# Graph attention and two graph convolutions on one Trainium2 core: block sums moved on GpSimd, batch 15's lower block sums moved to VectorE, batch 14's last step by seven products

## The chip, the cores and the metric

The kernel runs on one core of a Trainium2 chip (trn2). A core has TensorE (the matrix engine, PE in the profile, with weight loads as PEld), VectorE (DVE), ScalarE (ACT), GpSimd (POOL) and SyncE (SP), which here issues nearly all DMAs. The metric is the device time of one execution in microseconds. All data are float32.

## The reference

For 16 batches of x (1024 nodes, 256 channels) and one dense 1024 x 1024 matrix `adj`:

```python
c_adj = mean of x over channels                          # per node
A     = 2*| |sigmoid(c_adj[m]-c_adj[n]) - 0.5| - 0.5 |   # symmetric in n, m
g     = relu((x^T @ (adj * A)) * para)                   # [256, 1024], per batch
q     = g^T in 4 heads;  k, v = x @ kv_w
att   = softmax(q k^T * scale) v
x1    = layernorm(x + att)
h     = relu(x1 @ w1_loop + adj @ (x1 @ w1_neigh) + b1)  # 128 wide
h     = relu(h @ w2_loop + adj @ (h @ w2_neigh) + b2)    # 256 wide
out   = layernorm(x1 + 0.5*(x1 + h))
```

The last layernorm is over x1 + (x1 + h)/2; the kernel computes it as x1 + h/3 with the epsilon scaled to match.

## The kernel before

Each batch passes three stages on different turns of the loop over b, so that three or four batches are under way at once: the attention of batch b; the adjacency products of batch b+1 for its queries (`q`, class FastQueries); and the two convolutions. A GraphConv object stands for a batch whose attention is done: `c1` is batch b-1, `c2` is b-2, `c3` is b-3. The class Joined takes the first convolution's product of `c1` and the second one's of `c2` as one product with the same `adj`.

Where two 2 x 2 blocked matrices are multiplied, the kernel uses a scheme of seven products instead of eight (Winograd's form). It needs sums of blocks of each factor. Those concerned here are:

- `FastQueries.left` (L604 to L610): four sums of blocks of x, tiles `S`, 128x512 each, for the query products L647 of the next batch; its engine is an argument.
- `Joined.left` (L1120 to L1129): four sums, tiles `R`, for the joined product L1134. The first reads only `h1` of c2; the other three read `t`, the result of c1's small product (L857, copied from PSUM by ScalarE at L860).
- `GraphConv.block_sums` (L953 on): sums of blocks for the last step of c2, which multiplies [u, h1] by the weights w2 (L971, seven groups of four matmuls, `last_products`). Its first sum (L958) and the sum `uT` of the lower half (L1174) run on GpSimd, the rest on VectorE. The sums of the weights come by a DMA, `load_sums` (L950), which is issued from `Joined.run` after the second product.

Before the change the last pass (c1 of batch 15 and c2 of batch 14, after the loop) runs the joined product without `block_sums`, and then `c2.last()`: 16 matmuls of 256 columns into two PSUM tiles (`outer`, L926 and L928) and four long VectorE steps (`residual`, L933 and L936). `ending` then reuses these two PSUM tiles (`filled`) for batch 15.

All is in an order written by hand: an engine runs its instructions in the order of the program. Tiles named "row" (128 x 1024) rotate among 31 addresses: a new tile gets the address that was given back longest ago, and its first writer waits until the last readers of the former tile are done. So the order in which tiles are taken in the program sets which former tile a new one waits for. PSUM has three tiles of two banks ("big", of which `half_psum` uses one half) and two of one bank (`bank_psum`). Batch tiles of x rotate among three addresses (`xpool`): the load of batch 15's x1 (`c1.load_x`, L850) waits until the output of batch 12 (L1018) has left its tile.

In a steady batch (b = 2 to 14) the order around the change is: softmax sums of units 0 and 1 on VectorE (`collect` L721 and L723, `partial` L728 to the tile `accB`, L731 to `den_part`), `both.fetch`, the outputs of both units on PE (L744), `q.left`, the statistics of c3, the sums K of the next keys (L423 to L431), the adj loads, `c1.inner` (`t`), `both.left`, `both.run`.

In batch 15 `both.run` also holds batch 15's own normalisation: its power on GpSimd (L361) is put before the lower block sums.

Of the kernel before, what the change touches and what calls it, by code (L numbers as in the profile page):

```python
# [18 lines left out]
def kernel(  # L19
# [31 lines left out]
    nc = tc.nc  # L51

    B, N, C = x.shape
# [6 lines left out]
    FB = 512  # L60
# [781 lines left out]
    class GraphConv:  # L842
# [51 lines left out]
            nc.sync.dma_start(out=self.h1.rearrange("p (t f) -> p t f", f=HID),  # L894
                              in_=self.h1d.rearrange("(t p) f -> p t f", p=P))

        def turn(self, j):

            if j == 0:
                self.h1 = row_tile(f"h1_{self.b}")  # L900
            pt = half_psum(f"h1n_ps_{self.b}_{j}")
            for i in range(TJ):
                nc.tensor.transpose(pt[:, ts(i, P)], self.h1T[:, ts(j * TJ + i, P)], ident)
            nc.scalar.copy(self.h1[:, ts(j, FB)], pt)
# [45 lines left out]
            nc.sync.dma_start(out=self.w2[:, 0:5 * P], in_=w2_sums)  # L950
            self.b2_step = self.w2[:, ts(4, P)]

        def block_sums(self, base, lower):  # L953
            s12, s34 = (row_tile(f"last_{self.b}_{k}") for k in range(2))
            self.low, self.up = self.uT[:, FB:N], self.uT[:, 0:FB]
            s1, s2, s3, s4 = s12[:, 0:FB], s12[:, FB:N], s34[:, 0:FB], s34[:, FB:N]
            lower()
            nc.gpsimd.tensor_add(s1, self.h1T[:, FB:N], self.low)  # L958
            base()
            nc.vector.tensor_sub(s2, s1, self.up)  # L960
            nc.vector.tensor_sub(s4, self.h1T[:, 0:FB], s2)
            nc.vector.tensor_sub(s3, self.up, self.low)
            t1, t2, t3, t4 = (self.w2[:, ts(n, P)] for n in range(4))
            self.factors = {1: (self.up, w2n_sb[:, ts(0, P)]), 2: (self.h1T[:, 0:FB], w2l_sb[:, ts(0, P)]),
                            3: (s4, w2l_sb[:, ts(1, P)]), 4: (self.h1T[:, FB:N], t4), 5: (s1, t1), 6: (s2, t2), 7: (s3, t3)}
# [137 lines left out]
    class Joined:  # L1103
# [30 lines left out]
                nc.tensor.matmul(dst, self.x[n][:, k, :], of_rows(rows, k),  # L1134
                                 start=(start and k == 0), stop=(k == TJ - 1), skip_group_check=again)

        def run(self, between=None, last=False):
            c1, c2, b = self.c1, self.c2, self.b
            between = between or {}

            def bias(bank, row):
                nc.scalar.copy(bank.rearrange("p (t c) -> p t c", c=P), row.unsqueeze(1).to_broadcast([P, TJ, P]))

            def turn_to(n):
                for f in between.get(n, ()):
                    f()

            first, third, second = (half_psum(f"hu_ps_{b}_{i}") for i in range(3))
            s12, s34 = (row_tile(f"snap_{b}_{k}") for k in range(2))
            p1, u1, u3, p7 = s12[:, 0:FB], s12[:, FB:N], s34[:, 0:FB], s34[:, FB:N]  # L1150
            c1.loop(third, 0, start=True)
            self.product(1, first, start=True)
            nc.scalar.copy(p1, first)
            turn_to(1)
            self.product(2, third)
            nc.vector.tensor_add(p1, p1, third)
            turn_to(2)
            if last:
                bias(third, b2_sb[:, ts(0, P)])
                c2.load_sums()  # L1160
            self.product(6, first, again=True)
            nc.scalar.copy(u1, first)
            c1.relu(0, p1)
            turn_to(6)
            self.product(7, second, start=True)
            nc.scalar.copy(p7, second)
            turn_to(7)
            self.product(5, first, again=True)
            nc.scalar.copy(u3, first)
            turn_to(5)  # L1170
            self.product(4, second, again=True)
            c2.uT = row_tile(f"uT_{c2.b}")
            add_upper = lambda: nc.vector.tensor_add(c2.uT[:, 0:FB], u1, second)
            add_lower = lambda: nc.gpsimd.tensor_add(c2.uT[:, FB:N], u3, p7)  # L1174
            if not last:
                add_upper()
                add_lower()
                turn_to(4)
                c1.loop(first, 1, again=True)
                self.product(3, first, again=True)  # L1180
                c1.relu(1, first)
                turn_to(3)
                return
            c2.block_sums(add_upper, add_lower)
            bias(second, c2.b2_step)
            turn_to(4)
            c1.loop(first, 1, again=True)
            self.product(3, first, again=True, steps=range(0, TJ // 2))
            rest = c2.last_products(third, second)
            self.product(3, first, again=True, steps=range(TJ // 2, TJ))  # L1190
            c1.relu(1, first)
            rest()
            turn_to(3)

    def run():

# [57 lines left out]
        for b in range(B):  # L1254
# [39 lines left out]
            elif more and not both:  # L1294
                att.scores(0)
                att.outputs(0)
                NodeSums(q, xb, str(b + 1)).all()
                kv = KeysValues(b + 1, channel_major(blocked, f"xT_{b + 1}"))
                att.scores(1)
                kv.sums()  # L1300
                att.add(0)
                att.outputs(1)
                for t in (0, TJ):
                    q.load(t)
                c1.inner()
                q.left(nc.gpsimd)
                for t in (0, TJ):
                    q.likeness(t)
                for ij, n in QUARTERS.items():
                    store(n, quarters[ij])  # L1310
                c1.first(quarters, lambda: (att.add(1), adj_sums(quarters, 1), adj_sums(quarters, 2), weigh_first()))
                c1.turn_blocks()
                att.scores(2)
                att.outputs(2)
                for t in (1, TJ + 1):
                    q.load(t)
                    q.likeness(t)
                    q.times_adj(t)
                att.scores(3)
                for t in (2, TJ + 2, 3, TJ + 3):  # L1320
                    q.load(t)
                for t in (2, TJ + 2, 3, TJ + 3):
                    q.likeness(t)
                q.right(1)
                att.add(2)
                att.outputs(3)
            elif more:
                att.both_scores(0, summed=False)
                nodes = NodeSums(q, xb, str(b + 1))
                att.collect(1, 1, 2, 3)  # L1330
                nodes.turn()
                att.collect(1, *range(4, NT))
                att.partial(1)
                both.fetch("00", "10")
                c2.load_x()

                def next_xT():
                    ready["xT"] = channel_major(blocked, f"xT_{b + 1}")

                two_units(0, before_second=next_xT)  # L1340
                q.left(nc.gpsimd)
                if c3:
                    c3.statistics()
                kv = KeysValues(b + 1, ready["xT"])
                kv.sums()
                both.fetch(2, 3)
                nodes.line()
                both.fetch(1)
                nodes.row()
                for t in (0, TJ):  # L1350
                    q.load(t)
                both.fetch(4, "11")
                c1.inner()
                both.left(nc.gpsimd)
                both.run({1: (lambda: q.likeness(0),),
                          2: (lambda: att.add(0, 1), lambda: q.likeness(TJ), lambda: c3 and c3.deviation(), weigh_first)},
                         last=True)
                c1.turn_blocks()
                att.both_scores(1)
                order = (1, TJ + 1, 2, TJ + 2, 3, TJ + 3)  # L1360
                for t in order:
                    q.load(t)
                for t in order:
                    q.likeness(t)

                def weigh_second():
                    q.times_adj(1)
                    q.times_adj(TJ + 1)
                    q.right(1)

                two_units(1, before_second=weigh_second)
            else:
                att.both_scores(0)
                two_units(0)
                att.both_scores(1)
                two_units(1, before_second=lambda: att.add(0, 1))
# [58 lines left out]
            else:  # L1435
# [3 lines left out]
                both.left(nc.gpsimd)  # L1439
                both.fetch(1, 4, "11")  # L1440
                both.run({1: (lambda: att.add(2, 3), att.watch), 6: (norm.mean, norm.squares, norm.sum_squares),
                          5: (lambda: norm.variance(bank_psum),), 4: (norm.scale, norm.spread)}, last=True)
                c1.turn(0)
                c1.turn(1)
            convs[b] = GraphConv(b, norm.x1T, norm.nodes)
# [7 lines left out]
        c4.moments()  # L1453
        c4.finish(out[B - 4])
        c1.load_x()
        both.run({2: (c3.moments,), 7: (lambda: c3.finish(out[B - 3]),), 4: (lambda: c1.turn(0),)})
        filled = c2.last()
        c1.turn(1)
        c2.moments()
        c1.ending(out[B - 1], quarters, lambda: c2.finish_aside(out[B - 2]), filled)  # L1460
# [70 lines left out]
```

## Time and profile before

| | us |
|---|---|
| median of 3 runs (2158.33 to 2158.8) | 2158.66 |
| the profiled execution, whole | 2157.34 |
| its span | 2155.6 |
| a steady batch, start of L361 to start of the next (524.61 to 657.16) | 132.55 |
| PE, first record after product 4 in the last pass to its last matmul of batch 15 (2112.70 to 2146.5) | 33.8 |

The table of slices on the page shows PE and its clock even from end to end:

```profile
PE   9999999999999999999999999999999999999998
...
PEclk9999999999999999999999999999999999999999
DMA  8495765637539275492845929467293672935545
```

The operations that the change touches stand in the costliest groups (line, engine, operation, out<-in, shapes, count | busy us, mean ns of one | idle before them and what ended it):

```profile
L606 POOL TENSOR_TENSOR S<-x 128x512 f32<-128x512 f32 x14 | 25.1, 1794 | 258.2 <-ACT x L286 127.0 <-PE av L744 90.0 <-DMA x1d<-xB_a 23.1
L608 POOL TENSOR_TENSOR S<-x 128x512 f32<-128x512 f32 x14 | 30.6, 2183 | 0.0
L1126 POOL TENSOR_TENSOR R<-R,t 128x512 f32<-128x512 f32 x14 | 17.9, 1276 | 77.9 <-ACT t L860 77.9
L1174 POOL TENSOR_TENSOR uT<-snap 128x512 f32<-128x512 f32 x15 | 22.1, 1473 | 30.6 <-ACT snap L1169 30.6
L958 POOL TENSOR_TENSOR last<-h1T,uT 128x512 f32<-128x512 f32 x14 | 21.7, 1548 | 1.1
```

Idle time of an engine that does not bound the kernel costs nothing by itself; it tells what an instruction waited for.

### The profile page before, as it was taken

To read this page: it belongs to the slowest core of one execution; us is meant where nothing else is said; L and a number is where in the kernel's file an instruction comes from. 1 tells how busy PE (TensorE), PEld (TensorE's weight loads), DVE (VectorE), ACT (ScalarE), POOL (GpSimd) and SP (SyncE) were. 2 spreads that over 40 slices of the span, in tenths; PEclk is the share of its full clock that TensorE was granted. 3 is DMA by queue.
4 is the path that set the end of the run, shared out by engine and by line. 5 is a ranking of instruction groups with operands and counts; after the bars stand their busy time and mean duration, and the time that the engine had idled before them with its cause. 6 is when DMAs were issued, how large, how long until landed. Compare 5 with 4: busy or idle time off the path is not lost. (4 is left out here: it accounts for less than half of the span.)

```text
span 2155.6 us, 25079 instructions
## 1 busy us (share of the span) xinstructions
PE 2121.1 (98%) x8710; PEld 1035.5 (48%) x8710; DVE 1898.0 (88%) x2373; ACT 1138.2 (53%) x1664; POOL 391.8 (18%) x210
## 2 busy tenths in 40 slices
PE   9999999999999999999999999999999999999998
PEld 5344444544444454444554444544445444544454
DVE  6899988989999898998989989899898998989965
ACT  5845535556365563655636556355564546545422
POOL 2010130311303113031130311303022130311021
PEclk9999999999999999999999999999999999999999
DMA  8495765637539275492845929467293672935545
GB/s 220 124 163 199 131 213 138 183 97 151 207 110 268 78 146 192 128 269 69 168 163 135 261 69 198 141 152 235 69 230 109 159 228 69 258 94 120 163 136 179
DMA packets 613573, 346.05 MB, mean 161 GB/s; under 512 B 491968, under 2 KB 556864, under 8 KB 613440
## 3 DMA queue, kind: packets, MB, share of 16 engines
q1 hardware_dynamic: 613168, 344.13, 61.3%
q8 instruction: 70, 1.15, 0.2%
q14 instruction: 63, 0.52, 0.1%
q10 hardware_dynamic: 272, 0.26, 0.0%
HBM read 294.13 MB, written 50.20 MB: 160 GB/s over the span
## 5 line engine op out<-in xcount | busy, mean ns | idle before, releaser
L723 DVE TENSOR_TENSOR acc<-acc,pr 128x1024 f32<-128x1024 f32 x384 | 531.1, 1383 | 37.4 <-DVE acc L723 1.4
L702 PE MATMUL s<-qT,kT 64*128 64x512 f32 x2048 | 449.7, 593 | 0.0
L744 PE MATMUL av<-pr,v 128*64 128x512 f32 x2048 | 447.0, 594 | 0.0
L709 ACT ACTIVATE pr<-s 128x1024 f32<-128x1024 f32 x392 | 390.7, 1115 | 75.6 <-PE s L702 75.6
L702 PEld LDWEIGHTS s<-qT,kT 64*128 64x128 f32 x2048 | 196.3, 187 | 232.7 <-issue 183.3
L361 POOL TENSOR_TENSOR rstd<-rstd,neg_half 128x32 f32<-128x32 f32 x16 | 99.3, 6204 | 1112.7 <-DVE rstd L359 1112.7
L744 PEld LDWEIGHTS av<-pr,v 128*64 128x64 f32 x2048 | 144.0, 137 | 297.3 <-issue 272.6
L1134 PE MATMUL hu_ps<-adj,R 128*128 128x512 f32 x480 | 214.2, 594 | 0.0
L560 ACT ACTIVATE wg<-c_row,c_sums 128x1024 f32<-128x1024 f32 x120 | 137.0, 1142 | 81.4 <-DVE den_part L731 60.3
L566 DVE SCALAR_TENSOR_TENSOR wg<-wg,adj 128x1024 f32<-128x1024 f32 x128 | 149.9, 1210 | 3.6 <-ACT wg L561 3.6
L707 ACT ACTIVATE pr<-s 128x512 f32<-128x512 f32 x240 | 142.4, 702 | 0.3 <-PE s L702 0.3
L1134 PEld LDWEIGHTS hu_ps<-adj,R 128*128 128x128 f32 x480 | 89.1, 190 | 101.4 <-issue 98.3
L561 ACT ACTIVATE wg<-wg 128x1024 f32<-128x1024 f32 x128 | 135.4, 1058 | 4.1
L860 ACT COPY t<-t_ps 128x1024 f32<-128x1024 f32 x16 | 16.2, 1012 | 219.1 <-DVE den_part L731 190.3
L1134 PE MATMUL hu_ps<-adj,t 128*128 128x512 f32 x240 | 108.7, 605 | 21.5 <-ACT t L860 21.5
L647 PE MATMUL g_ps<-wg,S 128*128 128x512 f32 x224 | 115.5, 597 | 0.0
L647 PE MATMUL g_ps<-T,S 128*128 128x512 f32 x224 | 115.5, 597 | 0.0
L647 PE MATMUL g_ps<-wg,x 128*128 128x512 f32 x224 | 109.0, 599 | 0.0
L721 DVE TENSOR_TENSOR acc<-pr,pr 128x1024 f32<-128x1024 f32 x64 | 78.4, 1225 | 12.3 <-ACT pr L709 12.3
L1134 PEld LDWEIGHTS hu_ps<-adj,t 128*128 128x128 f32 x240 | 45.1, 193 | 84.0 <-issue 46.7
L728 DVE STREAM_TRANSPOSE accB<-acc 128x1024 f32<-128x1024 f32 x64 | 79.7, 1245 | 2.2
L731 DVE TENSOR_REDUCE den_part<-accB 128x32 f32<-128x1024 f32 x64 | 78.1, 1220 | 2.2
(239 smaller groups left out, 3062.6 us busy)
## 6 DMA issues: line engine op xcount, KB each, us to landing
adj<-adjT SPq DMA_DIRECT2D x210, 512.0 KB
adj<-in_adj_dram SPq DMA_DIRECT2D x128, 512.0 KB
para<-in_L_gnn_para_dram SPq DMA_DIRECT2D x32, 512.0 KB
xB_a<-in_x_dram SPq DMA_DIRECT2D x128, 128.0 KB
x1d<-xB_a SPq DMA_DIRECT2D x128, 128.0 KB
x<-x1d SPq DMA_DIRECT2D x16, 1024.0 KB
xB<-in_x_dram SPq DMA_DIRECT2D x120, 128.0 KB
x<-in_x_dram SPq DMA_DIRECT2D x15, 1024.0 KB
```

The costliest lines, as they stand in the source:

```text
L361: nc.gpsimd.tensor_tensor(self.rstd, self.rstd, neg_half, ALU.pow)
L560: nc.scalar.activation(wg, self.c_row, AF.Abs, bias=self.c_col[:, t:t + 1], scale=-1.0)
L561: nc.scalar.activation(wg, wg, AF.Tanh, scale=-0.5 / C)
L566: nc.vector.scalar_tensor_tensor(wg, wg, 1.0, self.adj.pop(t), op0=ALU.add, op1=ALU.mult)
L647: nc.tensor.matmul(self.p[n], x_n[:, k, :], w_n, start=(k == 0), stop=(k == TJ - 1))
L702: nc.tensor.matmul(halves[s], self.kT[rows, pair, ts(mt, P)], self.qT[rows, pair, ts(j, FB)], start=True, stop=True)
L707: nc.scalar.activation(pr[:, ts(s, FB)], halves[s], AF.Exp)
L709: nc.scalar.activation(pr, ps, AF.Exp)
L723: nc.vector.tensor_add(self.acc, self.acc, prs[mt])
L728: nc.vector.transpose(accB, self.acc)
L744: nc.tensor.matmul(pav[s * HD:(s + 1) * HD, :], self.v[:, mt, pair * P + s * HD:pair * P + (s + 1) * HD], prs[mt][:, ts(s, FB)], start=(mt ...
L1134: nc.tensor.matmul(dst, self.x[n][:, k, :], of_rows(rows, k), start=(start and k == 0), stop=(k == TJ - 1), skip_group_check=again)
```

## The change

Three edits. In a steady batch `q.left` moves from behind the outputs of units 0 and 1 to behind `both.left`, so GpSimd makes R before S, and the program takes the tiles K, adj, `t` and R before S. In batch 15 the lower sum `uT` and the first block sum go to VectorE (`last` is now the engine of these two). In the last pass the joined product runs with `last=nc.gpsimd`: batch 14's last step goes by `block_sums` and the seven groups of `last_products`, with the weight sums loaded by `load_sums`; `run` hands back its PSUM tiles `third` and `second` in the place of `filled`, and the first turn of h1 takes a one-bank PSUM tile.

```diff
-        def turn(self, j):
+        def turn(self, j, psum_tile=half_psum):
...
-            pt = half_psum(f"h1n_ps_{self.b}_{j}")
+            pt = psum_tile(f"h1n_ps_{self.b}_{j}")
...
-        def block_sums(self, base, lower):
+        def block_sums(self, eng, base, lower):
...
             lower()
-            nc.gpsimd.tensor_add(s1, self.h1T[:, FB:N], self.low)
+            eng.tensor_add(s1, self.h1T[:, FB:N], self.low)
...
-        def run(self, between=None, last=False):
+        def run(self, between=None, last=None):
...
-            add_lower = lambda: nc.gpsimd.tensor_add(c2.uT[:, FB:N], u3, p7)
+            add_lower = lambda: (last or nc.gpsimd).tensor_add(c2.uT[:, FB:N], u3, p7)
...
-            c2.block_sums(add_upper, add_lower)
+            c2.block_sums(last, add_upper, add_lower)
...
             turn_to(3)
+            return third, second
...
                 two_units(0, before_second=next_xT)
-                q.left(nc.gpsimd)
...
                 both.left(nc.gpsimd)
+                q.left(nc.gpsimd)
...
-                         last=True)
+                         last=nc.gpsimd)
...
-                          5: (lambda: norm.variance(bank_psum),), 4: (norm.scale, norm.spread)}, last=True)
+                          5: (lambda: norm.variance(bank_psum),), 4: (norm.scale, norm.spread)}, last=nc.vector)
...
-        both.run({2: (c3.moments,), 7: (lambda: c3.finish(out[B - 3]),), 4: (lambda: c1.turn(0),)})
-        filled = c2.last()
+        filled = both.run({2: (c3.moments,), 7: (lambda: c3.finish(out[B - 3]),), 4: (lambda: c1.turn(0, bank_psum),)},
+                          last=nc.gpsimd)
```

## The prediction

> **What bounds the kernel now.** I read the page first, then the waits of the matmul engine (PE), then the chain of waits, then timelines of one steady batch (batch 4, 524.6 to 657.2 us) and of the last 100 us. The page says who sets the pace:
>
> ```profile
> PE 2121.1 (98%) x8710; PEld 1035.5 (48%) x8710; DVE 1898.0 (88%) x2373; ACT 1138.2 (53%) x1664; POOL 391.8 (18%) x210
> ```
>
> At 98% PE can gain only by doing less or by losing its few waits. The waits of PE are (total us, times, longest):
>
> ```profile
> PE hu_ps L1134 <- ACT t L860: 21.5, 13, 3.5
> PE hu_ps L971 <- DVE h L993: 2.2, 1, 2.2
> ...
> PE hu_ps L971 <- issue: 0.4, 1, 0.4
> ```
>
> Thirteen waits for the copy of `t`: one in each batch 2 to 14 (3.54 us in batch 2, 1.5 each in the other twelve). The chain of waits shows what is behind one (start, us, what; this is batch 11's copy of the pattern):
>
> ```profile
> 1474.88 1.23 DVE acc L721
> 1476.20 1.24 DVE acc L723
> 1477.54 2.11 DVE acc L723
> ...
> 1486.32 2.18 DVE acc L723
> 1488.52 1.25 DVE accB L728
> 1489.80 1.23 DVE den_part L731
> 1491.13 1.02 ACT t L860
> 1492.19 7.13 PE hu_ps L1134 x16
> ```
>
> The reader is to see two things: the adds jump from 1.24 to 2.1-2.2 us in the middle of a run, and ScalarE's copy of `t`, which has nothing to do with the softmax sums, starts when `den_part` ends. In the built program `t` sits at the address that `accB` of unit 1 had just before, and `den_part` is the last reader of `accB`. GpSimd's timeline in batch 4 explains the slow adds:
>
> ```profile
> 548.96 1.88 POOL L606 TENSOR_TENSOR S<-x 128x512 f32<-128x512 f32 x1 [18.01 <-ACT x L286]
> ...
> 557.45 2.25 POOL L1125 TENSOR_TENSOR R<-h 128x512 f32<-128x512 f32 x1
> 564.57 1.28 POOL L1126 TENSOR_TENSOR R<-R,t 128x512 f32<-128x512 f32 x1 [4.88 <-ACT t L860]
> ...
> 579.12 2.55 POOL L316 TENSOR_TENSOR rstd_g<-rstd_g,neg_half 128x8 f32<-128x8 f32 x1 [10.81 <-DVE rstd_g L315]
> ```
>
> The block sums of x (S) and the first R sum lie exactly beside the slow adds. R's second sum waits 4.88 us for `t` anyway, and after R GpSimd idles 10.81 us. Batch 15 has its own wait: its lower block sums queue behind a 5.44 us power on GpSimd, VectorE waits for them, and PE for VectorE:
>
> ```profile
> 2073.59 1.26 POOL L1174 TENSOR_TENSOR uT<-snap 128x512 f32<-128x512 f32 x1
> 2076.24 0.69 DVE L960 TENSOR_TENSOR last<-last,uT 128x512 f32<-128x512 f32 x1 [4.12 <-POOL last L958]
> 2084.76 1.16 PE L971 MATMUL hu_ps<-w2l_sb,last 128*128 128x128 f32 x8 [2.16 <-DVE h L993]
> ```
>
> **What the Trainium skill says.** "Perfetto Trace Analysis", Optimization Strategy: the same gap repeating on the engine that should be saturated can mean that there is not enough SBUF for the next tile. The trace agrees: 1.54 us, twelve times, by a tile's address. "SBUF — State Buffer", Who interferes with whom: a VectorE instruction with two SBUF inputs and a GpSimd one that reads SBUF block each other for a whole instruction; VectorE instructions with one SBUF input do not. The trace agrees: adds 1.24 to 2.2 us beside S, while the transposes beside R (565 us) keep 1.17. "DMA: Bandwidth & Descriptors", Queues, rings and completion order: descriptors of one issuing engine are consumed in ring order; no run here shows it yet, and it decides a cost below.
>
> **Part 1, S behind R in batches 2 to 14.** Removed: nothing. Moved: four GpSimd sums, no DMA, and the places at which tiles are taken. S is taken after `t` and R now, so each of these gets an address freed two tiles earlier: `t` that of unit 1's fourth probability tile. PE reads that around 554 us in batch 4 (unit 1's 32 matmul pairs run 550.5 to 557.4). PE's last `t_ps` matmul ends near 561.2 us, the copy takes 1.01, so `t` is there at 562.3; PE's two loop products end at 562.94. The wait of 1.54 is hidden whole, 3.54 likewise in batch 2: 3.54 + 12 x 1.5 = 21.5 us less.
>
> What could be late next is VectorE. It gets back its lost time: two adds of 1.72 and four of 2.20 (3.44 and 8.80 in the timeline) against 1.31 each beside no GpSimd work make 4.4 us lost; R's first sum stays beside them, 0.9, so 3.5 come back. S now runs at about 566 to 575 us, first beside one-input statistics (free), then beside the sums K and the normalisation of the attention, two-input instructions of 0.69. The one such pair that the trace shows (L622 beside uT, 1.64 against 0.69) costs 0.95; three or four of them 2.9 to 3.8, another 0.95 possible at uT. Bounds for S's new cost: 0 to 6, I take 3.5: a draw. The slack: VectorE was ready for `uT` (L1173) 0.76 us before product 4 released it and could end at 585.60; PE asks for `uT` at 588.84, or 587.30 with the gain. So 1.7 us of slack on top of the draw. The power L316 behind S wants to start at 579; S ends by 575. R's product 6 needs R's sums near 570; they end at 566.2. The adj loads get addresses freed earlier, never later. I take -21.5, bounds -22.5 and -19.
>
> **Part 2, batch 15's lower sums on VectorE.** Added there: 2 x 0.69, in the 3.32 us in which VectorE waits for product 4 before L1173; they need the copy that ends at 2068.4. Removed: the 4.12 us wait. `last` is then ready at 2072.9, not 2076.9; the scale and transposes queued behind (4.7 us) end near 2079, and L993 near 2081.3, when PE wants it at 2082.2. Both PE waits go: 0.42 + 2.16 = 2.6 us less; bounds -2.6 and -1.5 (a blocked power, 6.35 instead of 5.44).
>
> **Part 3, batch 14's last step by seven products.** Removed: 16 matmul pairs of 256 columns, 2118.28 to 2125.19, 6.91 us. Added: seven groups of four, 0.89 each (2074.66 to 2075.55), 6.23: -0.7 on PE. VectorE gets nine short steps for four long ones, ScalarE five copies. One more DMA is added, the weight sums w2, and its place on SP's queue decides:
>
> ```profile
> 2103.43 3.74 SPq L1018 DMA_DIRECT2D out_dram<-x  x1
> 2117.04 0.36 SPq L850 DMA_DIRECT2D x<-x1d  x1
> ```
>
> L850 (batch 15's x) waits 9.8 us for the output of batch 12 to land and give its buffer back; the new load is queued behind it. The DMA stream before it is full (us, ..., last columns DMA share and GB/s):
>
> ```profile
> 2112.00:2114.00 2.00, 2.00 (x9) 0.99 (x9) 1.58 (x4) 0.59 (x1) 0.00 (x0) 1.00 1.09 375
> ...
> 2116.00:2118.00 2.00, 2.00 (x6) 0.90 (x5) 0.00 (x0) 0.00 (x0) 0.00 (x0) 1.00 0.03 9
> 2118.00:2120.00 2.00, 2.00 (x10) 1.57 (x9) 0.00 (x0) 0.69 (x1) 0.00 (x0) 1.00 0.60 122
> ```
>
> So landing moves only with the stream's start, batch 15's stores: L366 at 2074.1 for 2078.18, 3.9 us earlier. In before's clock with part 1 taken out: L850 at 2113.1, w2 issued at 2113.5. By ring order it follows L850's 1.05 MB: in before that much had moved by 2122.5, 5.5 after issue; w2's 0.33 MB at 0.38 MB/us 0.9; last packet to semaphore 1.5 (2115.5 to 2117.04). It lands at 2121.0. Then ScalarE, in order: the bias from w2, the copy of h, the copy of p1, 1.7 us. PE wants group 6 at 2112.70 + 0.43 (turn) + 1.72 (loop) + 1.72 (half of product 3) + 2 x 0.89 = 2118.35, less 2.6: 2115.8. It gets it at 2122.7: a new PE wait of 6.9 us. Bounds: 3.5 (the three transfers share from the start) and 9.5 (w2 behind batch 13's output too). Net +6.2, bounds +2.8 and +8.8.
>
> **Sum.** -21.5 - 2.6 + 6.2 = -17.9. The profiled execution took 2157.34 (span 2155.6 and 1.7 around): 2139.4. The median of the runs is 1.3 above it: 2140.8.
>
> **Rivals.** (a) w2 comes in time: no wait, 2158.66 - 21.5 - 2.6 - 0.7 = 2133.9. For it: nothing shows the order inside the queues. Against: L850 is released only 2.7 us before PE's need, and its 1.05 MB move first. (b) S costs VectorE about 6 us, `uT` is late, half of part 1 is given back: -10.7 - 2.6 + 6.2, 2151.6. For it: K's adds are two-input; against: the 3.5 us returned. (c) The same place, slower than before: each S sum blocks VectorE longer than its own 1.27 us and nothing returns. With d us of net delay PE waits d - 1.7 at `uT`; with parts 2 and 3 the kernel is slower from d = 3.0; at d = 4.0, 13 x (2.3 - 1.54) + 3.6 = +13.5, 2172. It needs 6.5 us or more for four sums whose own time is 5.1. (d) The change does not do what it says, `t` waits for another late tile: -2.6 + 6.2, 2162.3; against: its new address is free 7 us before.
>
> **How the numbers follow.** Forecast 0.72 (2136 to 2146 by its bounds), (a) 0.11, (b) 0.10, (c) 0.04, (d) 0.03. The range 2133 to 2147 holds the forecast and (a), 0.83. A measurement of this kernel can tell about 0.2% (4.3 us) from nothing. Faster: forecast, (a), (b): 0.93; same: (d) at +0.17%: 0.03; slower: 0.04.
>
> **What would show it.** The waits of PE without the thirteen for `t`; unit 1's adds near 1.31 until R's first sum; L960 not waiting for GpSimd; one new PE wait near the end at L971's third group, ended by ScalarE's copy or w2's DMA, of about 7 us; L366 four us earlier against product 4. Wrong if PE waits for DVE uT in steady batches, or if the end shows no wait.

## The result, and the profile after

| | before | after |
|---|---|---|
| median, us | 2158.49 (4 runs, 2155.54 to 2158.80) | 2135.99 (4 runs, 2135.35 to 2137.19) |
| ratio, with 95% interval | | 0.9899 [0.9882, 0.9917] |
| span of the profiled execution | 2155.6 | 2133.6 |

The kernel became 22.5 us faster by the medians, 22.0 by the spans. The forecast was 2140.8, with a range of 2133 to 2147.

Where the 22 us are is read from the starts of PE's first `t_ps` matmul (L857) in each batch. Starts are used, not the waits that the profile lists: the end of a matmul is modelled, so a listed wait is only part of what a late start costs. A column named after a batch is that turn of the loop, from its first `t_ps` to the next turn's. The last column, here and below, runs from the first `t_ps` after the loop (batch 15's own) to the start of PE's last matmul.

| us | up to batch 2's `t_ps` | batches 2 to 14 | batch 4 alone | batch 15 | last pass |
|---|---|---|---|---|---|
| before | 288.65 | 1755.97 | 132.55 | 42.08 | 60.84 |
| after | 288.05 | 1729.34 | 130.74 | 39.10 | 68.96 |
| difference | -0.6 | -26.6 | -1.8 | -3.0 | +8.1 |

Three parts, three stretches: -26.6 for S behind R, -3.0 for batch 15, +8.1 for batch 14's last step, and -0.6 at the start. No part of the change touches the start; over all thirteen traces of this case it ends anywhere from 287.89 to 290.13 us.

The waits of PE after (engine, tile, line and what it waited for: total us, times, longest):

```profile
PE hu_ps L971 <- ACT h L984: 6.8, 1, 6.8
PE idle L1206 <- POOL ident masks.py:199: 1.5, 1, 1.5
PE good_ps L1475 <- DVE x L1054: 1.0, 1, 1.0
```

The thirteen waits for `t` and both waits of batch 15 are gone. One new wait stands in the last pass; the other two lines, at the very start and the very end, are in before too.

VectorE's timeline after, batch 4 (start us, us, engine, line, operation, out<-in, shapes, count):

```profile
540.62 2.56 DVE L723 TENSOR_TENSOR acc<-acc,pr 128x1024 f32<-128x1024 f32 x2
...
543.22 4.99 DVE L723 TENSOR_TENSOR acc<-acc,pr 128x1024 f32<-128x1024 f32 x4
548.25 1.25 DVE L728 STREAM_TRANSPOSE accB<-acc 128x1024 f32<-128x1024 f32 x1
549.53 1.22 DVE L731 TENSOR_REDUCE den_part<-accB 128x32 f32<-128x1024 f32 x1
550.66 0.71 DVE L755 STREAM_TRANSPOSE o<-av 128x512 f32<-128x512 f32 x1
...
558.36 1.69 DVE L423 TENSOR_TENSOR K<-xT 128x512 f32<-128x512 f32 x1
560.08 1.65 DVE L424 TENSOR_TENSOR K<-xT,K 128x512 f32<-128x512 f32 x1
561.65 1.76 DVE L430 TENSOR_TENSOR K<-xT 128x512 f32<-128x512 f32 x1
563.34 1.75 DVE L431 TENSOR_TENSOR K<-xT,K 128x512 f32<-128x512 f32 x1
```

The six adds of unit 1 that ran beside S are back at 1.25 to 1.28 us each. What slows now are the four sums K, 1.65 to 1.76 for 0.68. GpSimd's timeline in the same batch shows S exactly beside them:

```profile
554.55 1.27 POOL L1126 TENSOR_TENSOR R<-R,t 128x512 f32<-128x512 f32 x1 [5.21 <-ACT t L860]
...
558.23 1.27 POOL L606 TENSOR_TENSOR S<-x 128x512 f32<-128x512 f32 x1
559.58 1.61 POOL L607 TENSOR_TENSOR S<-S,x 128x512 f32<-128x512 f32 x1
561.14 1.72 POOL L608 TENSOR_TENSOR S<-x 128x512 f32<-128x512 f32 x1
562.83 1.71 POOL L609 TENSOR_TENSOR S<-x,S 128x512 f32<-128x512 f32 x1
```

And PE's timeline there has no number in brackets, that is, no wait: product 1 (L1134 with `t`) follows the loop product at once.

```profile
553.20 1.88 PE L864 MATMUL hu_ps<-x1T,w1l_sb 128*128 128x512 f32 x4
554.92 7.03 PE L1134 MATMUL hu_ps<-adj,t 128*128 128x512 f32 x16
```

The last pass after, in the timeline, from SP, ScalarE and PE:

```profile
2072.27 3.42 SPq L1018 DMA_DIRECT2D out_dram<-x  x1
2085.64 0.36 SPq L850 DMA_DIRECT2D x<-x1d  x1
2086.09 0.53 SPq L950 DMA_DIRECT2D w_sums<-w_sums  x1
...
2093.49 0.59 ACT L1142 COPY hu_ps<-w_sums 128x512 f32<-128x512 f32 x1 [13.65 <-DMA w_sums<-w_sums]
2094.01 0.58 ACT L904 COPY h<-h1n_ps 128x512 f32<-128x512 f32 x1
2094.49 0.59 ACT L984 COPY h<-hu_ps 128x512 f32<-128x512 f32 x1
...
2095.13 4.62 PE L971 MATMUL hu_ps<-w_sums,last 128*128 128x128 f32 x24 [6.83 <-ACT h L984]
```

The weight sums w2 (L950) are issued right behind L850, which is held until batch 12's output has landed. They arrive 7.8 us after L850's issue. ScalarE takes its three copies in order behind them, and PE waits 6.83 us. The 24 matmuls that follow take 4.62 us; the same groups take 2.98 in batch 15.

### The profile page after: what moved, and what is told of

Same layout as the page of the kernel before. It is cut to its first block, busy times and chain, and to the rows that moved or that the text cites. A ratio compares the mean times of both kernels' runs of the same rounds, so it can differ in the third digit from the quotient of the medians.

```text
span 2133.6 us, 25172 instructions
## 1 busy us (share of the span) xinstructions
PE 2116.3 (99%) x8734; PEld 1037.2 (49%) x8734; DVE 1907.5 (89%) x2381; ACT 1140.1 (53%) x1669; POOL 359.0 (17%) x209
## 4 chain that ended last, share of the span: by engine, by line
PE 98%; DMA 1%; DVE 1%; ACT 0%; POOL 0%; issue 0%; POOLq 0%; SPq 0%; ACTq 0%; DVEq 0%
PE s L702 21%; PE av L744 21%; PE g_ps L647 16%; PE hu_ps L1134 16%; PE v_ps L448 5%; PE k_ps L444 5%; PE hu_ps L971 4%; PE t_ps L857 3%; PE g_ps L574 3%; PE hu_ps L864 2%; PE h_ps L879 1%; PE u_ps L908 1%; DMA out_dram<-x 1%; PE h_ps L971 1%; DMA w_sums<-w_sums 0%; PE den_ps L764 0%
## 5 line engine op out<-in xcount | busy, mean ns | idle before, releaser
L723 DVE TENSOR_TENSOR acc<-acc,pr 128x1024 f32<-128x1024 f32 x384 | 472.2, 1230 | 37.4 <-DVE acc L723 1.4
L1134 PE MATMUL hu_ps<-adj,R 128*128 128x512 f32 x480 | 214.3, 594 | 0.0
L1134 PEld LDWEIGHTS hu_ps<-adj,R 128*128 128x128 f32 x480 | 89.0, 190 | 100.9 <-issue 99.5
L1134 PE MATMUL hu_ps<-adj,t 128*128 128x512 f32 x240 | 105.7, 592 | 0.0
L1125 POOL TENSOR_TENSOR R<-h 128x512 f32<-128x512 f32 x14 | 28.2, 2012 | 359.5 <-PE av L744 238.8
```

The lines of the kernel that those rows point to most:

```text
L723: nc.vector.tensor_add(self.acc, self.acc, prs[mt])
```

## The experiments

**1 to 4: the parts alone.** `e_left_only` is the kernel before with only the move of `q.left`:

```diff
                 two_units(0, before_second=next_xT)
-                q.left(nc.gpsimd)
...
                 both.left(nc.gpsimd)
+                q.left(nc.gpsimd)
```

> Part 1 alone: S behind R in batches 2 to 14, all else as before. Theory (the waits for t are worth their start-to-start loss, 1.81 us in twelve batches and 5.4 in batch 2): 26 to 27 us less, ratio near 0.9877, a steady batch of 130.74 us, no wait of PE for ScalarE's t. Rival (the waits are worth what the list of waits names, 21.5 us, and the rest of the gain comes from parts 2 and 3): ratio near 0.990.

`e_b15_only` is the kernel before with the engine of the two lower sums as an argument, VectorE in batch 15:

```diff
-            nc.gpsimd.tensor_add(s1, self.h1T[:, FB:N], self.low)
+            eng.tensor_add(s1, self.h1T[:, FB:N], self.low)
...
-            add_lower = lambda: nc.gpsimd.tensor_add(c2.uT[:, FB:N], u3, p7)
+            add_lower = lambda: (last or nc.gpsimd).tensor_add(c2.uT[:, FB:N], u3, p7)
...
-                          5: (lambda: norm.variance(bank_psum),), 4: (norm.scale, norm.spread)}, last=True)
+                          5: (lambda: norm.variance(bank_psum),), 4: (norm.scale, norm.spread)}, last=nc.vector)
```

> Part 2 alone: batch 15's lower block sums on VectorE. Theory: the two PE waits of 0.42 and 2.16 us at L971 go, 2.6 to 3.0 us less, ratio near 0.9987, and the thirteen waits for t stay. Rival (the power on GpSimd is slowed beside VectorE's sums and gives the gain back): no change.

`e_last_only` is the kernel before with only the last pass changed, and `e_no_last` the changed kernel with the old last pass:

```diff
-        both.run({2: (c3.moments,), 7: (lambda: c3.finish(out[B - 3]),), 4: (lambda: c1.turn(0),)})
-        filled = c2.last()
+        filled = both.run({2: (c3.moments,), 7: (lambda: c3.finish(out[B - 3]),), 4: (lambda: c1.turn(0, bank_psum),)},
+                          last=nc.gpsimd)
```

> Part 3 alone: batch 14's last step by seven products, without parts 1 and 2. Theory (the weight sums w2 are queued behind L850, which waits for batch 12's output): L850 starts near 2117 us as before the change, w2 lands 7.8 us later, PE waits about 8 us at L971's third group and runs at half clock for some 3 us after it: 8 to 10 us slower, ratio near 1.004. It is worse here than in the whole change by 1 to 2 us, since part 2 starts the DMA stream earlier. Rival (seven for eight products gain 0.7 us and the wait is a matter of the whole change): ratio 0.9997.

> The change without part 3. Theory: parts 1 and 2 add up, 26.6 + 3.0 us less than before, near 2129 us, ratio near 0.986, about 8 us faster than the whole change; no wait of PE at the end. Rival (the end is bound by DMA or VectorE anyway, so that taking part 3 away moves the wait elsewhere): within 3 us of the whole change.

Measured, against the kernel before (2157.72 us in these runs; parts of the span by PE's starts as above):

| | median us | ratio, 95% interval | batches 2 to 14 | batch 15 | last pass |
|---|---|---|---|---|---|
| e_left_only | 2130.96 | 0.988 [0.9865, 0.9895] | 1729.35 | 42.08 | 61.05 |
| e_b15_only | 2154.39 | 0.9986 [0.998, 0.9993] | 1755.71 | 39.10 | 60.85 |
| e_last_only | 2167.17 | 1.0043 [1.0029, 1.0057] | 1754.27 | 42.48 | 69.93 |
| e_no_last | 2127.69 | 0.986 [0.9845, 0.9875] | 1729.34 | 39.10 | 60.84 |

Each part acts in its own stretch. The 1.7 us by which `e_last_only` differs from before in batches 2 to 14, and its 0.4 us in batch 15, are a matter of the clock (last section). Parts 1 and 2 add up: -26.8 and -3.3 us by the medians alone, -30.0 together. Part 3 loses: 9.4 us by itself, and without it the changed kernel is 8.3 us faster. Its expectation was off in one point: PE's listed wait in `e_last_only` is 6.49 us, not about 8, since PE comes to it later there (the 32 `t_ps` matmuls of the last pass take 4.91 us for 3.84). The trace of `e_last_only` is of an execution of 2164.24 us, 2.9 below its median; what the others add is not shown.

**5 and 6: what PE waited for in the steady batches.** The prediction had `t` wait because its address was `accB`'s, last read by `den_part`. Two kernels split this from GpSimd's load on VectorE. `e_t_bound_first` is the kernel before with S still ahead of R, but `t` takes its address before S does (a one-column write binds it), so it no longer follows `accB`:

```diff
+                c1.t_tile = row_tile(f"t1_{c1.b}")
+                nc.scalar.copy(c1.t_tile[:, 0:1], ones_sb)
                 q.left(nc.gpsimd)
```

> Kernel before, but t gets its address before S (one ScalarE copy of a single column binds it, before S is taken; the full copy L860 overwrites it). S stays in its old place beside VectorE's adds. Address theory: the adds stay at 2.1 to 2.2 us and den_part as late as before, yet the thirteen waits go: 25 to 27 us less, ratio near 0.988. Contention theory (the slowed adds hold PE up whatever address t has): the waits stay, ratio 1.000.

`e_s_bound_old` is the reverse: S runs behind R, but its two tiles are bound where they were, so `t` keeps `accB`'s former address:

```diff
-                q.left(nc.gpsimd)
+                q.left_tiles()
...
                 both.left(nc.gpsimd)
+                q.left(nc.gpsimd)
```

> S runs behind R as in the change, but its two tiles are bound to addresses in the old place (two ScalarE copies of a single column, overwritten by S), so t gets accB's address as before the change. Contention theory: the adds of unit 1 fall to about 1.3 us, den_part ends 3 us earlier, before PE's last t_ps matmul, and the waits go as well: ratio near 0.988. Address theory alone: t still waits for den_part, ratio 1.000. If both kernels of this pair lose the waits, each half of part 1 is enough by itself.

Measured (before: 2158.1): `e_t_bound_first` 2152.38, ratio 0.9974 [0.9964, 0.9984]; `e_s_bound_old` 2132.51, 0.9881 [0.9866, 0.9896]. Of the 21.5 us of listed waits at product 1 the first keeps 16.4, the second none. For the first, neither theory fits: it gains 5.7 us, where one asked for 25 to 27 and the other for nothing. So the address is not what has to go: with it unchanged the waits vanish once S is away from the adds, and with another address most of the wait stays. The timeline of `e_t_bound_first`, batch 4 (lines below L846 are one further down than in before):

```profile
557.58 1.25 DVE L728 STREAM_TRANSPOSE accB<-acc 128x1024 f32<-128x1024 f32 x1
...
557.83 1.88 PE L865 MATMUL hu_ps<-x1T,w1l_sb 128*128 128x512 f32 x4
558.09 1.01 ACT L861 COPY t<-t_ps 128x1024 f32<-128x1024 f32 x1 [12.36 <-PE t_ps L858]
...
558.86 1.22 DVE L731 TENSOR_REDUCE den_part<-accB 128x32 f32<-128x1024 f32 x1
...
559.99 0.71 DVE L755 STREAM_TRANSPOSE o<-av 128x512 f32<-128x512 f32 x1
...
560.80 1.53 PE L1135 MATMUL hu_ps<-adj,t 128*128 128x512 f32 x3 [1.09 <-issue]
```

`t` is there at 559.10, before PE could go on at 559.55 (1.72 us after its loop product started, as in after). Yet PE starts at 560.80, just as VectorE ends its transpose L755. In the built program the first tile of the joined product (`first`) takes the PSUM bank in which unit 0's output `av` was, and L755 is its last reader. It stands right behind `den_part` on VectorE. In the kernel before the two waits nest: L755 ends at 563.93 and `t` comes at 564.43, and the trace names only the later one, `t`.

**7: both at once.** `e_t_turn_early` adds one move to `e_t_bound_first`: unit 1's `partial`, which makes `accB` and `den_part`, goes behind the transpose of unit 0's output.

```diff
-                att.partial(1)
...
                 def next_xT():
...
+                    att.partial(1)
```

> The kernel before with t bound ahead of S, as in e_t_bound_first, and the turn of unit 0's output on VectorE (the transpose of av, last reader of the PSUM tile that the joined product's first tile takes) put ahead of unit 1's last sums accB and den_part instead of behind them. S stays ahead of R, so the adds stay slow (2.2 us each beside GpSimd). Theory 'two late readers': in e_t_bound_first the wait that stayed was for that PSUM tile. With the transpose some 2.5 us earlier (about 557.5 instead of 560 in batch 4) the PE's joined product starts when t's copy ends, the thirteen waits go, and the time is about 20 to 26 us below the kernel before: ratio 0.988 to 0.991, about 2133 to 2138 us. Rival 'VectorE is late anyway': what S costs VectorE is then asked for at the next place, uT, and PE waits there; the time stays near that of e_t_bound_first, ratio 0.996 to 0.998, 2150 to 2154 us.

It took 2131.68 us, ratio 0.9878 [0.9861, 0.9894], just under the range expected, with batches 2 to 14 in 1729.7 us (2018.38 - 288.66): all that the change won there. VectorE's adds are as slow as before:

```profile
545.51 8.79 DVE L723 TENSOR_TENSOR acc<-acc,pr 128x1024 f32<-128x1024 f32 x4
554.23 0.70 DVE L755 STREAM_TRANSPOSE o<-av 128x512 f32<-128x512 f32 x1
...
556.09 1.22 DVE L731 TENSOR_REDUCE den_part<-accB 128x32 f32<-128x1024 f32 x1
```

So the waits need two things together: VectorE late by S, and two tiles (`t` in SBUF, `first` in PSUM) given back by VectorE after those adds. Taking away the lateness (run 6) frees PE, and so does having both tiles free early enough although VectorE is late (run 7); moving `t` alone (run 5) does not. Freeing `first` alone was not tried.

**8 and 9: w2 earlier.** Both are the changed kernel with one call moved. `e_w2_before_x` issues the load right ahead of L850; `e_w2_first` ahead of the last adj loads.

```diff
         both.fetch("00", "10", 2, 3, 1, 4, "11")
+        c2.load_sums()
         quarters = fetch_quarters("e", both.far)
```

> The whole change, but w2's load stands just ahead of L850 on SP's queue, behind batch 12's output. Theory: w2 is issued near 2076 us and, by ring order, lands with the end of the full DMA stream near 2085; ScalarE's bias waits until then, PE's wait at L971's third group is under 1 us: 8 to 9 us less than the change, near 2128 us, ratio to before near 0.986. Rival (the wait comes from the bandwidth of the last 10 us, not from the queue's order): a wait of several us stays.

> The whole change, but w2's load stands ahead of the last pass's other small loads, behind its seven adj products. Theory: w2 lands before it is asked for, ScalarE's bias waits for VectorE's uT only, no wait of PE at the end: near 2128 us, ratio to before near 0.986, 0.5 to 1 us faster than the change without part 3. Rival: the earlier load delays adj tiles of the last pass and PE waits for these.

They took 2127.51 (0.9858 [0.9843, 0.9873]) and 2127.14 us (0.9857 [0.9842, 0.9872]), against 2158.1 before. The wait is gone in both. `e_w2_first` is ahead of the changed kernel by 2135.99 - 2127.14 = 8.9 us. By the medians it is level with `e_w2_before_x`, and its lead of 0.55 us on `e_no_last` (2127.69) is no more than the spread of the runs. In the traces its last pass takes 60.33 us, 0.5 less than the 60.84 with the old step: that is what seven products are worth when their weights are there. How near `e_w2_before_x` comes to a wait is seen in its timeline (the load from SP, and the first copy behind it on ScalarE):

```profile
2073.23 3.35 SPq L1019 DMA_DIRECT2D out_dram<-x  x1
2076.68 4.64 SPq L951 DMA_DIRECT2D w_sums<-w_sums  x1
2086.79 0.36 SPq L851 DMA_DIRECT2D x<-x1d  x1
...
2087.64 0.59 ACT L1143 COPY hu_ps<-w_sums 128x512 f32<-128x512 f32 x1 [6.85 <-DMA w_sums<-w_sums]
```

w2 is issued at 2076.68 and lands only 11 us later, at 2087.6: 0.8 us after batch 12's output, whose landing releases L851. "DMA: Bandwidth & Descriptors", Queues, rings and completion order, has each DMA engine consume its descriptors in ring order, and these landings agree: w2 stays behind the transfer that was issued ahead of it.

**10 and 11: why the last pass cost more than its wait.** The granted clock, the share of its full speed that TensorE was allowed, suggests why groups 6, 5 and 7 took 4.62 us. After, by windows (columns: window, us, busy of PE, PEld, DVE, ACT, POOL, clock, DMA share, GB/s):

```profile
2091.00:2092.00 1.00, 0.00 (x0) 0.00 (x0) 0.00 (x0) 0.00 (x0) 0.00 (x0) 0.92 1.04 379
2092.00:2098.00 6.00, 2.87 (x13) 2.87 (x14) 1.38 (x2) 2.18 (x4) 0.00 (x0) 0.50 0.48 170
2098.00:2099.00 1.00, 1.00 (x8) 1.00 (x7) 0.00 (x0) 0.00 (x0) 0.00 (x0) 0.66 0.00 0
```

`e_pe_kept_busy` is the changed kernel with matmuls that nobody reads between groups 2 and 6, so that PE is busy while it waits:

```diff
+            for k in range(13 if spare is not None else 0):
+                nc.tensor.matmul(spare, ident, self.h1T[:, 0:FB], start=True, stop=True, skip_group_check=True)
             self.seventh_part(6, a)
```

> The changed kernel with 13 more matmuls (identity by batch 14's h1, 128x512, some 0.43 us each) on PE between groups 2 and 6 of batch 14's last step, into an unused half of a PSUM tile; nobody reads them. They fill about 5.6 us of the 6.8 us in which PE waits for w2, and change nothing of what it waits for. Theory 'half clock': the wait costs more than its length since the granted clock falls to 0.50 in it and the next groups 6, 5, 7 run at it. With PE busy the clock stays at 1.00, the 24 matmuls of groups 6, 5, 7 take 3.0 us as in batch 15 instead of 4.62, the listed wait shrinks to about 1.2 us, and the last pass is 1.6 us shorter (68.96 to about 67.4 from batch 15's first t_ps to the last matmul); about 2134.4 us. Rival 'slow groups': groups 6, 5, 7 are held by the copies of h and the PSUM banks that they share, the clock is only beside it; they stay at 4.5 us or more and the last pass at 68.9 to 69.1.

The 13 were mis-sized: each is two instructions and they ran 11.32 us, past w2's arrival, for 2138.08 us (0.9912 [0.9895, 0.9928]). But groups 6, 5, 7 took 2.89 us at clock 1.00. So with 7:

> As e_pe_kept_busy, with 7 matmuls in the place of 13: each is two instructions and took 0.86 us there, not 0.43, so 13 of them ran 11.3 us and overran the wait by 4.2 us. 7 make 6.0 us and end ahead of w2. Theory 'half clock': the listed wait is about 0.9 us, groups 6, 5, 7 take 2.9 us at clock 1.00 and start when they did before, so the last pass is 1.7 us shorter than the changed kernel's: 67.3 against 68.96; the time some 1.6 us below it, about 2134.4 us. Rival 'no gain': the groups start later by what they save, the last pass stays at 68.9 to 69.1.

It took 2133.33 us, 0.989 [0.9873, 0.9906], and its last pass 67.06 us (2123.61 - 2056.55), 1.9 less than the changed kernel's, by doing more work. Its ratio alone does not tell it from the changed kernel (0.9899 [0.9882, 0.9917]); the last pass does. PE in its timeline:

```profile
2088.21 6.17 PE L989 MATMUL hu_ps<-h1T,ident 128*128 128x512 f32 x14
2094.92 2.99 PE L971 MATMUL hu_ps<-w_sums,last 128*128 128x128 f32 x24 [0.54 <-ACT h L984]
2097.75 1.88 PE L1136 MATMUL hu_ps<-adj,R 128*128 128x512 f32 x4
```

The groups start as late as after, and take 2097.75 - 2094.92 = 2.83 us for 2099.59 - 2095.13 = 4.46. Of the 1.9 us, 1.63 are the clock; the rest is w2, 0.3 us earlier against PE. The rival theory, that copies and banks held these groups, falls.

## Why the prediction was right, and where it was off

The case that the prediction put first came about: the waits for `t` go, batch 15's go, one new wait for w2 of about 7 us comes. The terms of all three parts had the right sign, and each was too small:

| us | predicted | measured |
|---|---|---|
| part 1, S behind R | -21.5 | -26.6 |
| part 2, batch 15 | -2.6 | -3.0 |
| part 3, last step by seven products | +6.2 | +8.1 |
| start, up to batch 2 | none | -0.6 |
| sum | -17.9 | -22.1 |

Part of the hit is luck. The measured terms of parts 1 and 2 lie outside the prediction's own bounds (-22.5 to -19, and -2.6 to -1.5), and the errors, -5.1, -0.4, +1.9 and -0.6, partly cancel. The 2135.99 us stand at the very edge of the 2136 to 2146 that the forecast gave itself. By the time alone rival (a), 2133.9, is nearer than 2140.8; what speaks against it is the wait of 6.83 us in the trace, where (a) has none.

**Part 1, the size.** The term "3.54 + 12 x 1.5" took the waits as the profile lists them. Start to start, from the loop product to product 1, batch 4 went from 564.48 - 561.06 = 3.42 us to 554.92 - 553.20 = 1.72, and the batch from 132.55 to 130.74: 1.81, not 1.54. Over the other twelve batches this is (26.6 - 5.4) / 12 = 1.77 on average. Batch 2 lost 5.44 us, not 3.54 (136.18 before, 130.74 after), since in this execution its wait also halved the clock, and product 1 took 8.77 us for 7.13. Before, by windows of a microsecond:

```profile
297.00:298.00 1.00, 0.25 (x1) 0.25 (x2) 1.00 (x2) 0.70 (x1) 0.16 (x1) 0.83 1.03 389
298.00:299.00 1.00, 1.00 (x2) 0.48 (x3) 1.00 (x2) 0.00 (x0) 1.00 (x1) 0.50 1.02 418
...
301.00:302.00 1.00, 1.00 (x3) 0.38 (x2) 1.00 (x1) 0.00 (x0) 1.00 (x1) 0.96 1.01 414
```

**Part 1, the cause.** The steps "so each of these gets an address freed two tiles earlier" and "The wait of 1.54 is hidden whole" reach the right end by an incomplete way. A new address alone left most of the wait (run 5), and the old address did no harm (run 6). What the move of S brought was VectorE on time at this place, and that time the prediction booked only as a draw. "Perfetto Trace Analysis", Optimization Strategy, speaks of SBUF and PSUM for such a repeating gap; the prediction took up the first alone, and runs 5 and 7 show both.

**Part 1, the cover.** The prediction had 3.5 us come back to VectorE and 3.5 spent by S at its new place. In batch 4 4.7 came back (3.44 - 2.56 and 8.80 - 4.99), and the K sums cost 6.85 - 2.72 = 4.1 more: S falls on them whole, not in part on the statistics as forecast. One more sum beside uT is slow as well: L620 and L621 take 1.64 and 1.75 after, where only L622 took 1.64 before. That makes 5.1, still about a draw. VectorE is now later for `uT` than PE's product 4: L1173 ends at 578.28 and PE uses `uT` at 579.17. 0.9 us of slack is left where 1.7 was forecast. Rivals (b) and (c) needed a net delay beyond that slack; it was 0.4. Rival (d) fell with run `e_left_only`.

**Part 2.** Both waits went, 2.6 by the list; start to start 3.0. VectorE's L366, which starts the stores of batch 15, comes 2.66 us after L1173 for 6.75 before: 4.1 us earlier, where 3.9 was forecast.

**Part 3.** The order of the queue was foreseen: w2 landed 7.8 us after L850's issue, where the working gave 7.9. The wait of 6.83 us stands beside 6.9. Groups 6, 5, 7 would have started at 2087.25 + 0.89 = 2088.14 and started at 2095.13: 7.0. Seven products gained 0.5, not 0.7. The missing term is the half clock behind the wait, 1.63 us: -0.5 + 7.0 + 1.6 = +8.1. "TensorE: Matmul & The Clock Gate", Why this matters for your kernels, warns of idle gaps over about 3 us between matmuls; this trace agrees, with 0.50 granted from 2091.84, 3.7 us after PE ran out of work, to 2098.67, 3.5 us after work resumed. Shorter gaps can do the same, as the last section shows. Rival (a) is what runs 8 and 9 made of the change.

## What to carry to other kernels

When an engine waits for something late, list everything that the late engine gives back in that stretch, PSUM banks too: the trace names only the last. Count a wait start to start, and where PE idles 2 us or more allow for the matmuls behind it at half clock. Before a step is given a new operand, look at what its load is queued behind, and issue it ahead of a transfer that waits for a buffer.

## What the runs showed of the hardware that was not expected

- Half clock behind an idle stretch has a price of its own: 1.63 us here, and keeping PE busy with matmuls that nobody reads won it back (`e_pe_busy_7`).
- The length of a wait does not decide it alone. The wait of 3.54 us in batch 2 halved the clock in before, and left it at 1.00 in `e_last_only` (product 1 7.13 us), so 1.6 of part 1's 26.6 us were this execution's. The wait of 2.16 us in batch 15 (L993) left it at 1.00 in before, and in `e_last_only` the same 2.16 us were followed by 3.4 us at half clock. The 32 `t_ps` matmuls took 4.91 us there and 3.84 in before, which is 1.07 of the 9.1 us that its last pass lost. Batch 15 of `e_t_bound_first` and of `e_t_turn_early` (43.65 and 43.59 us for 42.08) is 1.5 us longer with the clock at 0.50 behind the same wait.
- What decides can be read from the traces. Apart from the start and the end of a trace, every stretch of half clock lasts 3.41 us or twice that (before 297.67 to 301.08, `e_last_only` 2083.69 to 2087.10, after 2091.84 to 2098.67), and the changes of the clock in one trace lie whole multiples of 3.413 us apart (301.08 to 2151.10 in before: 542 of them). Cut into such stretches, a trace shows PE's busy time in each and the clock in the next. First before, then `e_last_only`, both at the wait of 2.16 us:

```profile
2082.84:2086.25 3.41, 1.49 (x13) 1.49 (x14) 3.34 (x6) 0.00 (x0) 0.00 (x0) 1.00 0.99 147
2086.25:2089.66 3.41, 3.41 (x31) 3.26 (x30) 1.78 (x3) 1.07 (x2) 0.00 (x0) 1.00 0.90 177
...
2080.27:2083.69 3.42, 1.38 (x12) 1.38 (x13) 3.35 (x7) 0.00 (x0) 0.00 (x0) 1.00 0.98 144
2083.69:2087.10 3.41, 3.41 (x18) 3.41 (x17) 1.89 (x3) 1.17 (x2) 0.00 (x0) 0.50 0.98 183
```

| wait of PE (us) | stretch of 3.41 us | PE busy in it | clock in the next |
|---|---|---|---|
| before, batch 2 (3.54) | 294.25 to 297.67 | 0.00 | 0.50 |
| `e_last_only`, batch 2 (3.54) | 291.69 to 295.10 | 1.76 | 1.00 |
| the same wait | 295.10 to 298.52 | 1.53 | 1.00 |
| `e_t_bound_first`, batch 15 (2.15) | 2073.13 to 2076.55 | 1.27 | 0.50 |
| `e_t_turn_early`, batch 15 (2.16) | 2055.00 to 2058.41 | 1.37 | 0.50 |
| `e_last_only`, batch 15 (2.16) | 2080.27 to 2083.69 | 1.38 | 0.50 |
| before, batch 15 (2.16) | 2082.84 to 2086.25 | 1.49 | 1.00 |
| `e_left_only`, batch 15 (2.16) | 2053.90 to 2057.31 | 1.59 | 1.00 |

In all thirteen traces half clock follows every stretch with PE busy for at most 1.38 us, and full clock every one with at least 1.49. So, as an estimate from these numbers, a wait costs extra where it takes about 2 us out of one such stretch. Where the stretches lie against the program differs from execution to execution: the wait of 3.54 us fills one stretch in before and is split over two in `e_last_only`. The twelve waits of 1.54 us were too short for it; no stretch of before around them has PE busy for less than 1.86 us. The ends of matmuls are modelled, and nothing was run to place the limit between 1.38 and 1.49 more closely.
